# Giving each DMA engine an output region of its own in a bilinear-pairs kernel

## The chip, the cores and the metric

The kernel runs on one core of one Trainium2 chip. A core has five engines that run side by side: TensorE (PE, with its weight loads shown as PEld), VectorE (DVE), ScalarE (ACT), GpSimd (POOL) and SyncE (SP). Sixteen DMA engines move data between DRAM (HBM) and the core's on-chip memory (SBUF), which has 128 partitions. The metric is the time of one execution on the device, in microseconds (us). Before the change it is 766.56 us, the median of three runs (766.03 to 769.45). The profiled execution took 771.7 us, of which its profile spans 769.8.

## The reference

There are 1024 batch rows with 32 fields of 128 values each, and one 128 x 128 matrix for each of the 496 pairs of fields i < j. For every pair the first field's vector is multiplied by the pair's matrix, and the result, element by element, by the second field's vector:

```
v_i = inputs[:, I_IDX, :]
v_j = inputs[:, J_IDX, :]
transformed = jnp.einsum('bpd,ped->bpe', v_i, W)
return transformed * v_j
```

All is float32. The output has 1024 x 496 x 128 elements, 260 MB; the inputs have 17 MB (fields) and 33 MB (matrices). The kernel may choose its own layout in DRAM: the host only permutes axes before and after.

## The kernel before

**Layout.** The host hands the fields over as `xt` (128 elements d, 32 fields, 1024 batch rows) and the matrices as `wt`, four pairs to a block (124 blocks of 128 d x 4 pairs x 128 e). The output in DRAM is `(248, 128, 2, 1024)`: 248 groups g of two pairs (`OG = 2`), and in each group 128 rows e, one for each SBUF partition, of 2 pairs x 1024 batch rows. A group is thus one contiguous megabyte, and each partition's share of it, 8 KB, is contiguous too.

**Work.** Pairs are taken with i from 30 down to 0. A unit u is one pair q and one half h of the batch (512 rows). It has two parts:

- `first(u)` multiplies the pair's matrix with the field into a PSUM tile `po`. The first 15 pairs (`NATIVE = 5`) do so in one plain float32 matmul (L154). All others use a split in a rounded high part, a low part and a correction: two matmuls in the format float32r (L157), and then ScalarE scales the tile in place (L158).
- `second(u)`, `LAG = 3` units later, adds the third matmul (L166) and lets VectorE multiply `po` with the second field into the output tile `ot` (L172).

`split_w` (L94 to L97, ScalarE and GpSimd) and `split_x` (L109 to L115, and L195 on VectorE) make the parts. They are placed in the loop by a list with due times.

**Transfers.** The loop is written out in order (a manual schedule), and SyncE issues nearly all DMAs in it, in the order of the program: W blocks (256 KB, four blocks ahead), fields (512 KB), and after the fourth unit of each group the whole tile `ot[g]` (1 MB, L176). Only the last two pairs go out in four pieces of 256 KB (L174). Four `ot` tiles exist; VectorE can begin a group only once the output DMA of the fourth group before has landed.

**What the change touches.** Lines L174 and L176 name the target of the output DMAs; the rest is the declaration of the output tensor and the host's permutation after the run.

Of the kernel before, what the change touches and what calls it, by code (L numbers as in the profile page):

```python
# [1 line left out]

# [4 lines left out]

F32 = mybir.dt.float32
F32R = mybir.dt.float32r
ALU = mybir.AluOpType  # L10

P = 128
NF = 32
NQ = NF * (NF - 1) // 2
BT = 1024
HB = 512
WC = 2
WL = 4
OG = 2
EPS = 2.0**-12  # L20
NATIVE = 5
SHARED = 10
XDLAG = 10
LAG = 3
WLEAD = 4
XLEAD = 5


def _pairs():

    return [(i, j) for i in range(NF - 2, -1, -1) for j in range(i + 1, NF)]


@with_exitstack
def kernel(
    ctx: ExitStack,
    tc: tile.TileContext,
    xt: bass.AP,
    wt: bass.AP,
    out: bass.AP,  # L40
):

    nc = tc.nc
    pairs = _pairs()
    nchunk = NQ // WC  # L60

    xpool = ctx.enter_context(tc.tile_pool(name="x", bufs=1))
    spool = ctx.enter_context(tc.tile_pool(name="xs", bufs=2))
    rpool = ctx.enter_context(tc.tile_pool(name="wr", bufs=5))
    wpool = ctx.enter_context(tc.tile_pool(name="ws", bufs=4))
    opool = ctx.enter_context(tc.tile_pool(name="o", bufs=4))
    ppool = ctx.enter_context(tc.tile_pool(name="ps", bufs=8, space=bass.MemoryType.PSUM))

    x_sb = {}

    def load_x(f, n=1, pieces=1, eng=None):

        t = xpool.tile([P, n, BT], F32, tag=f"x{f}", name=f"x_{f}")
        s = BT // pieces
        for k in range(pieces):
            (eng or nc.sync).dma_start(out=t[:, :, k * s : (k + 1) * s], in_=xt[:, f : f + n, k * s : (k + 1) * s])
        for k in range(n):
            x_sb[f + k] = t[:, k, :]

    w_raw = {}  # L80

    def load_w(c, splits=(0, WL)):
        w_raw[c] = rpool.tile([P, WL, P], F32, tag="w", name=f"w_{c}")
        for a, b in zip(splits, splits[1:]):
            nc.sync.dma_start(out=w_raw[c][:, a:b, :], in_=wt[c, :, a:b, :])  # L85

    w_s = {}

    def split_w(c, u):

        k = c * WC % WL
        raw = w_raw[c * WC // WL][:, k : k + WC, :].rearrange("p q e -> p (q e)")
        h, l, d = [wpool.tile([P, WC * P], F32R, tag=t, name=f"{t}_{c}") for t in ("wh", "wl", "wd")]
        nc.scalar.mul(h, raw, 1.0 - 2.0**-13)  # L94
        nc.gpsimd.tensor_tensor(l, raw, h.bitcast(F32), ALU.subtract)  # L95
        nc.gpsimd.tensor_scalar(d, h.bitcast(F32), EPS, 1.0, ALU.mult, ALU.mult)  # L96
        nc.gpsimd.tensor_tensor(d, l.bitcast(F32), d.bitcast(F32), ALU.subtract)  # L97
        w_s[c] = (h, l, d)

    x_s = {}  # L100
    later = []

    def split_x(f, a, u):

        if a == 0:
            x_s[f] = [spool.tile([P, BT], F32R, tag=t, name=f"{t}_{f}") for t in ("xh", "xl", "xd")]
        s = slice(a, a + HB)
        h, l, d = [t[:, s] for t in x_s[f]]
        nc.scalar.mul(h, x_sb[f][:, s], 1.0 - 2.0**-13)  # L109
        nc.gpsimd.tensor_tensor(l, x_sb[f][:, s], h.bitcast(F32), ALU.subtract)  # L110
        nc.gpsimd.tensor_scalar(l, l.bitcast(F32), 1.0 / EPS, 1.0, ALU.mult, ALU.mult)  # L111
        if f > NF - 2 - NATIVE - SHARED:
            later.append((min(u + XDLAG, 2 * first_q[f] + LAG - 1), d, h.bitcast(F32), l.bitcast(F32)))
        else:
            nc.gpsimd.tensor_tensor(d, h.bitcast(F32), l.bitcast(F32), ALU.subtract)  # L115

    nq0 = NATIVE * (NATIVE + 1) // 2
    c0 = nq0 // WC
    first_q = {i: q for q, (i, j) in reversed(list(enumerate(pairs)))}

    todo = []
    for c in range(c0, nchunk):
        todo.append(((c - 3) * WC + 1, max(c * WC, nq0), lambda u, c=c: split_w(c, u)))
    for i in range(NF - 2 - NATIVE, -1, -1):
        for a in range(0, BT, HB):
            todo.append((first_q[i + 1] + 1 if i < NF - 3 - NATIVE else 2, first_q[i], lambda u, i=i, a=a: split_x(i, a, u)))
    todo.sort(key=lambda t: t[1])

    load_w(0, (0, 1, WL))
    load_x(NF - 2, pieces=2, eng=nc.scalar)
    load_x(NF - 1, pieces=2, eng=nc.scalar)
    load_x(NF - 3)
    load_x(NF - 4)
    load_w(1)
    for f in range(NF - 5, NF - 4 - XLEAD, -1):
        load_x(f)
    load_w(2)
    load_w(3)  # L140


    ctx.enter_context(tc.manual_schedule())
    po, ots = {}, {}


    def first(u):
        q, h = divmod(u, 2)
        i, c = pairs[q][0], q // WC
        r = slice(q % WC * P, (q % WC + 1) * P)  # L150
        s = slice(h * HB, (h + 1) * HB)
        po[u] = ppool.tile([P, HB], F32, tag="po", name=f"po_{u}")
        if q < nq0:
            nc.tensor.matmul(po[u], w_raw[q // WL][:, q % WL, :], x_sb[i][:, s], start=True, stop=True)  # L154
        else:
            for t in (0, 1):
                nc.tensor.matmul(po[u], w_s[c][t][:, r], x_s[i][t][:, s], start=t == 0, stop=t == 1)  # L157
            nc.scalar.mul(po[u], po[u], 1.0 + EPS)  # L158

    def second(u):  # L160
        q, h = divmod(u, 2)
        i, j = pairs[q]
        r = slice(q % WC * P, (q % WC + 1) * P)
        s = slice(h * HB, (h + 1) * HB)
        if q >= nq0:
            nc.tensor.matmul(  # L166
                po[u], w_s[q // WC][2][:, r], x_s[i][2][:, s], start=False, stop=True, skip_group_check=True
            )
        g, k = divmod(q, OG)
        if k == 0 and h == 0:  # L170
            ots[g] = opool.tile([P, OG, BT], F32, tag="ot", name=f"ot_{g}")
        nc.vector.tensor_tensor(ots[g][:, k, s], po.pop(u), x_sb[j][:, s], ALU.mult)  # L172
        if q >= NQ - 2:
            nc.sync.dma_start(out=out[g, :, k, s], in_=ots[g][:, k, s])  # L174
        elif k == OG - 1 and h == 1:
            nc.sync.dma_start(out=out[g], in_=ots[g])  # L176

    for u in range(2 * NQ + LAG):
        q = u // 2
        if u % (2 * WL) == 0 and (q // WL + WLEAD) * WL < NQ:  # L180
            load_w(q // WL + WLEAD)
        if u < 2 * NQ:
            i, j = pairs[q]
            if u % 2 == 0 and j == i + 1 and 0 <= i - 2 - XLEAD:
                load_x(i - 2 - XLEAD)
            first(u)
        if u >= LAG:
            second(u - LAG)
        if u % 2 == 1:
            ready = [t for t in todo if t[0] <= q]  # L190
            if ready:
                ready[0][2](u)
                todo.remove(ready[0])
        while later and later[0][0] <= u:
            nc.vector.tensor_tensor(*later.pop(0)[1:], ALU.subtract)  # L195
    assert not todo and not later


# [25 lines left out]
```

## Time and profile before

| | before |
|---|---|
| time, median of 3 | 766.56 us |
| span of the profile | 769.8 us |
| PE busy | 722.7 us (94%) |
| VectorE busy | 632.0 us (82%) |
| ScalarE busy | 638.7 us (83%) |
| GpSimd busy | 593.2 us (77%) |
| moved by the DMA engines | 310.11 MB, mean 403 GB/s |
| written to HBM, read from it | 260.05 MB, 49.28 MB |
| an output DMA (1 MB), issue to landing | 8.9 us |

PE's busy time is modelled, since matmuls overlap in the array. The page's second part cuts the span into 40 equal slices; a digit is the busy share in tenths, and the line named DMA is the mean over the sixteen DMA engines. The third part gives each DMA queue's share of these engines' time. The fourth follows the work that ended last back to the start; a share of it for a DMA means that something waited for that transfer. The fifth groups instructions by line. A packet is the piece that one DMA engine moves at a time, one 8 KB partition row for the output; the trace has a record of each packet's start, length and size.

### The profile page before, as it was taken

The page shows a single profiled execution, that of the slowest core. Times are in us where ns is not written, and L with a number is a line of the kernel's source. Part 1 is how long each engine was busy: PE and PEld are TensorE (multiplying, and loading weights), DVE is VectorE, ACT ScalarE, POOL GpSimd, SP SyncE. Part 2 cuts the span into 40 slices and gives each one's busy share as a digit, 9 for nine tenths or more (in the row PEclk, how much of TensorE's full clock was granted, in tenths as well). Part 3 has the DMA queues.
Part 4 walks back from the last instruction along what each step waited for, and adds up shares of the span by engine and source line. Part 5 has one row for each costly group of instructions (what it writes and reads, how often), then busy time and mean ns, then how long its engine had stood idle before and what let it go on. Part 6 is the DMA issues. An engine that isn't in the chain of part 4 may idle for free.

```text
span 769.8 us, 11824 instructions
## 1 busy us (share of the span) xinstructions
PE 722.7 (94%) x2946; PEld 545.4 (71%) x2946; DVE 632.0 (82%) x1012; ACT 638.7 (83%) x1256; POOL 593.2 (77%) x863
## 2 busy tenths in 40 slices
PE   7988999999999999999999989999999999999994
PEld 3556766677777676777777767777777777777773
DVE  4869888888888788888888878888888888888885
ACT  2276988888888898888888889998988898998983
POOL 2677998887889878878878696978786969697660
PEclk9999999999999999999999999999999999999998
DMA  9999999999999999999999999999999999999997
GB/s 352 424 419 384 407 397 410 405 400 406 410 405 403 400 409 416 409 379 421 411 414 407 412 403 406 411 407 408 415 410 395 408 410 409 409 408 405 400 401 307
DMA packets 59108, 310.11 MB, mean 403 GB/s; under 512 B 6560, under 2 KB 6816, under 8 KB 27424
## 3 DMA queue, kind: packets, MB, share of 16 engines
q1 hardware_dynamic: 58464, 308.31, 99.4%
q10 hardware_dynamic: 576, 1.05, 0.4%
q8 instruction: 24, 0.39, 0.2%
q14 instruction: 44, 0.36, 0.1%
HBM read 49.28 MB, written 260.05 MB: 402 GB/s over the span
## 4 chain that ended last, share of the span: by engine, by line
DMA 61%; DVE 21%; PE 15%; issue 2%; DVEq 0%; SPq 0%; ACT 0%
DMA out_dram<-ot 60%; DVE ot L172 19%; PE po L157 9%; PE po L166 4%; DVE xd L195 2%; PE po L154 1%; DMA x<-in_xt_dram 1%; DVEq L172 0%; SPq L85 0%; DVEq L217 0%; ACT po L158 0%; DVEq L195 0%
## 5 line engine op out<-in xcount | busy, mean ns | idle before, releaser
L172 DVE TENSOR_TENSOR ot<-po,x 128x512 f32<-128x512 f32 x992 | 618.6, 684 | 129.5 <-DMA out_dram<-ot 70.2
L158 ACT ACTIVATE po<-po 128x512 f32<-128x512 f32 x962 | 551.2, 583 | 106.5 <-PE po L157 53.3
L157 PE MATMUL po<-xh,wh 128*128 128x512 f32 x962 | 388.7, 404 | 24.4 <-DVE ot L172 21.6
L166 PE MATMUL po<-xd,wd 128*128 128x512 f32 x962 | 376.9, 392 | 5.7 <-DVE xd L195 5.7
L157 PE MATMUL po<-xl,wl 128*128 128x512 f32 x962 | 377.6, 392 | 2.2 <-POOL wl L95 2.1
L157 PEld LDWEIGHTS po<-xh,wh 128*128 128x128 f32 x962 | 180.9, 188 | 110.2 <-DVE ot L172 72.5
L95 POOL TENSOR_TENSOR wl<-w,wh 128x256 fp32r<-128x256 f32 x241 | 179.2, 744 | 92.1 <-ACT wh L94 90.7
L166 PEld LDWEIGHTS po<-xd,wd 128*128 128x128 f32 x962 | 181.0, 188 | 46.3 <-ACT po L158 3.8
L157 PEld LDWEIGHTS po<-xl,wl 128*128 128x128 f32 x962 | 181.1, 188 | 36.8 <-POOL wl L95 4.5
L97 POOL TENSOR_TENSOR wd<-wl,wd 128x256 fp32r<-128x256 f32 x241 | 180.0, 747 | 20.1
L96 POOL TENSOR_SCALAR wd<-wh 128x256 fp32r<-128x256 f32 x241 | 99.1, 411 | 20.3
L94 ACT ACTIVATE wh<-w 128x256 fp32r<-128x256 f32 x241 | 99.2, 412 | 0.5 <-DMA w<-in_wt_dram 0.5
L110 POOL TENSOR_TENSOR xl<-x,xh 128x512 fp32r<-128x512 f32 x52 | 67.3, 1293 | 19.8 <-ACT xh L109 19.5
L115 POOL TENSOR_TENSOR xd<-xh,xl 128x512 fp32r<-128x512 f32 x32 | 41.4, 1292 | 2.7
L109 ACT ACTIVATE xh<-x 128x512 fp32r<-128x512 f32 x52 | 32.5, 628 | 10.5 <-DMA x<-in_xt_dram 10.3
L111 POOL TENSOR_SCALAR xl<-xl 128x512 fp32r<-128x512 f32 x52 | 32.8, 631 | 4.6
L154 PE MATMUL po<-x,w 128*128 128x512 f32 x60 | 29.0, 645 | 4.1 <-DMA x<-in_xt_dram 4.1
L154 PEld LDWEIGHTS po<-x,w 128*128 128x128 f32 x60 | 12.1, 206 | 20.2 <-issue 13.9
L195 DVE TENSOR_TENSOR xd<-xh,xl 128x512 fp32r<-128x512 f32 x20 | 16.6, 831 | 0.0
L109 ACT ACT_TABLE_LOAD x1 | 1.3, 1283 | 2.6 <-issue 2.6
L211 POOL MEMSET const-float32-0.0<- 128x1 f32 x1 | 0.1, 98 | 0.2 <-issue 0.2
L211 POOL MEMSET const-bfloat16-1.0<- 128x1 bf16 x1 | 0.1, 101 | 0.0
(2 smaller groups left out, 0.2 us busy)
## 6 DMA issues: line engine op xcount, KB each, us to landing
out_dram<-ot SPq DMA_DIRECT2D x247, 1024.0 KB, 8.9
w<-in_wt_dram SPq DMA_DIRECT2D x123, 256.0 KB, 9.1
x<-in_xt_dram SPq DMA_DIRECT2D x30, 512.0 KB, 9.5
x<-in_xt_dram ACTq DMA_DIRECT2D x4, 256.0 KB, 5.1
out_dram<-ot SPq DMA_DIRECT2D x4, 256.0 KB, 7.0
w<-in_wt_dram SPq DMA_DIRECT2D x1, 192.0 KB, 3.6
w<-in_wt_dram SPq DMA_DIRECT2D x1, 64.0 KB, 2.9
```

Source lines behind the costliest of these rows:

```text
L94: nc.scalar.mul(h, raw, 1.0 - 2.0**-13)
L95: nc.gpsimd.tensor_tensor(l, raw, h.bitcast(F32), ALU.subtract)
L96: nc.gpsimd.tensor_scalar(d, h.bitcast(F32), EPS, 1.0, ALU.mult, ALU.mult)
L97: nc.gpsimd.tensor_tensor(d, l.bitcast(F32), d.bitcast(F32), ALU.subtract)
L109: nc.scalar.mul(h, x_sb[f][:, s], 1.0 - 2.0**-13)
L110: nc.gpsimd.tensor_tensor(l, x_sb[f][:, s], h.bitcast(F32), ALU.subtract)
L115: nc.gpsimd.tensor_tensor(d, h.bitcast(F32), l.bitcast(F32), ALU.subtract)
L154: nc.tensor.matmul(po[u], w_raw[q // WL][:, q % WL, :], x_sb[i][:, s], start=True, stop=True)
L157: nc.tensor.matmul(po[u], w_s[c][t][:, r], x_s[i][t][:, s], start=t == 0, stop=t == 1)
L158: nc.scalar.mul(po[u], po[u], 1.0 + EPS)
L166: nc.tensor.matmul(po[u], w_s[q // WC][2][:, r], x_s[i][2][:, s], start=False, stop=True, skip_group_check=True)
L172: nc.vector.tensor_tensor(ots[g][:, k, s], po.pop(u), x_sb[j][:, s], ALU.mult)
```

## The change

The output tensor becomes two-dimensional: 16 regions (`NE`), each of 3,968 x 1024 floats (15.5 MB) followed by a padding of 9 x 1024 floats (36 KB) that nobody writes. Region n holds partitions 8n to 8n+7 of every group, group after group. So one output DMA writes 64 KB into each of the sixteen regions, and in a region the next group follows directly on the one before. The purpose is that each of the sixteen DMA engines writes into a region of its own, in one continuous stream over the whole run, with regions that start at different offsets. Tiles, order of work, sizes of DMAs and arithmetic stay the same; the host undoes the new layout.

```diff
+NE = 16
+PAD = 9 * BT
...
         if q >= NQ - 2:
-            nc.sync.dma_start(out=out[g, :, k, s], in_=ots[g][:, k, s])
+            nc.sync.dma_start(out=out[:, g, :, k, s], in_=ots[g][:, k, s])
         elif k == OG - 1 and h == 1:
-            nc.sync.dma_start(out=out[g], in_=ots[g])
+            nc.sync.dma_start(out=out[:, g], in_=ots[g])
...
-    args.append(nc.dram_tensor("out_0_dram", (NQ // OG, P, OG, BT), F32, kind="ExternalOutput").ap())
+    own = NQ * P // NE * BT
+    whole = nc.dram_tensor("out_0_dram", (NE, own + PAD), F32, kind="ExternalOutput").ap()
+    args.append(whole[:, :own].rearrange("n (g e k b) -> n g e k b", g=NQ // OG, e=P // NE, k=OG))
...
-    y[:, perm, :] = got.transpose(3, 0, 2, 1).reshape(BT, NQ, P)
+    got = got[:, :own].reshape(NE, NQ // OG, P // NE, OG, BT)
+    y[:, perm, :] = got.transpose(4, 1, 3, 0, 2).reshape(BT, NQ, P)
```

## Prediction

> **What bounds the kernel now.** I read the page from its slices first, then the queues, the chain, the groups, and last the waits and two windows of the trace.
>
> ```profile
> DMA  9999999999999999999999999999999999999997
> GB/s 352 424 419 384 407 397 410 405 400 406 410 405 403 400 409 416 409 379 421 411 414 407 412 403 406 411 407 408 415 410 395 408 410 409 409 408 405 400 401 307
> DMA packets 59108, 310.11 MB, mean 403 GB/s; under 512 B 6560, under 2 KB 6816, under 8 KB 27424
> ...
> q1 hardware_dynamic: 58464, 308.31, 99.4%
> ...
> HBM read 49.28 MB, written 260.05 MB: 402 GB/s over the span
> ...
> DMA out_dram<-ot 60%; DVE ot L172 19%; PE po L157 9%; PE po L166 4%; DVE xd L195 2%; PE po L154 1%; DMA x<-in_xt_dram 1%; DVEq L172 0%; SPq L85 0%; DVEq L217 0%; ACT po L158 0%; DVEq L195 0%
> ...
> out_dram<-ot SPq DMA_DIRECT2D x247, 1024.0 KB, 8.9
> ```
>
> The reader is to see that all sixteen DMA engines are busy in every slice, that one queue fills 99.4% of their time, that 260 of 310 MB are the output, and that the output's DMAs are 60% of the chain. The kernel is bound by its transfers from start to end. The question for any change is therefore what it does to the time of one output packet. In the trace's records of single packets, the output goes in 31,664 packets of 8 KB: half of them take 309 ns, the mean is 319.8. That is 8192 B / 309 ns = 26.5 GB/s for each engine, and 424 GB/s for sixteen.
>
> The next bound lies close. A window late in the span, and the waits for output buffers:
>
> ```profile
> 500.00:600.00 100.00, 98.43 (x413) 76.02 (x412) 85.80 (x139) 90.44 (x179) 79.17 (x116) 1.00 1.01 408
> ```
>
> ```profile
> DVE ot L172 <- DMA out_dram<-ot: 70.2, 83, 2.1
> ```
>
> VectorE waits only 70.2 us in all for a free output buffer, and PE is 98.43% busy by the page's modelled ends. Matmuls start 0.227 us apart in the timeline, so 3 x 962 of them need 655 us, the 60 native ones at 645 ns 39 us; the chain's first matmul starts at 7.9 us, and the last output needs some 9 us to land: about 711 us is a floor under which no faster transfer takes the kernel.
>
> [...] The page counts eight packets to an engine and output DMA (31,664 / 247 / 16 = 8.0)[...]. No view shows which partition an engine reads[...].
>
> **The change, part by part.**
>
> *Bytes, packets and issues.* Still 247 DMAs of 1 MB and four of 256 KB at the end, from the same tiles in the same order. Each SBUF partition still holds 8 KB, so I expect the same 8 KB packets [...]: 0 us. The padding is never written: 0 us. If a DMA with two different shapes takes SyncE longer to issue, the queue hides it: an output lands 8.9 us after its issue, in a rhythm of two outputs per 5.78 us (VectorE's waits for a buffer in the timeline are at 610.10 and 615.89).
>
> *What the writes gain.* The most that a better DRAM layout can give is what packets take beyond their usual time: 31,664 x 10.8 ns / 16 = 21.3 us for the output, and 26.9 us with both kinds of loads. Some 17 us of this comes in short bursts, and late in the span these stand just ahead of a W load, where the engines turn from writing the output to reading; a new place for the output leaves that turn as it is. That leaves 10 us that could go. Value taken: 0 to 5 us, with 27 us as the outer end.
>
> *What DRAM can lose.* Sixteen streams now lie 15.5 MB + 36 KB apart. [...] Before, an output's sixteen shares all lay inside 1 MB. Value: 0, upper end 2% of the output's time (12 us).
>
> *Who reads which partitions.* This is the step on which I stake the forecast. The DRAM side's slowest dimension is now 16 and no longer 128. [...] Two engines [...] take about 2 x 309 = 618 ns for a packet.
>
> How much of the time partners are in step decides the size. [...] In the window from 600 to 606 us, in slices of 0.15 us, the bytes by start of packet go up and down:
>
> ```profile
> GB/s 601 218 614 177 683 137 737 109 492 273 109 68 273 478 369 423 751 232 519 232 628 232 601 273 601 218 601 218 655 164 655 218 601 273 546 328 492 382 492 382
> ```
>
> High and low alternate because most engines begin their packets in the same half of each 309 ns. Their offsets there are within half a packet; at 200 and 400 us they are spread over a whole one, with a few engines two to four packets ahead. [...]
>
> The output's packet time on one engine is 247 x 8 x 309 ns = 611 us; all of it lies on the bounding path, because the engines are never idle. Doubling all of it would add 611 us (1378 us). With a share of 0.5 it is 766.6 + 306 = 1073, with 0.87 it is 766.6 + 532 = 1299. Loads are untouched: their DRAM side keeps its shape. I take 0.7, as slow pairs hold up all others[...]: 766.6 + 0.7 x 611 = 1194, about 1195 us. VectorE would then wait for buffers at every output, PE behind it.
>
> **The rivals.**
>
> *No change (766 us).* [...] partners separate by four packets and stay so, and the DRAM layout was not limiting. For it: half of the packets are already at 309 ns, so the layout has little to mend. [...]
>
> *Faster (757 us).* One stream per engine removes the scattered part of the stalls, up to 10 us: 766.6 - 9.6. For it: mean above median by 10.8 ns per packet. Against it: most of the excess is at turns to a load.
>
> *Slightly slower (785 us).* Partners separate for the most part, with collisions left for some 3% of the output (611 x 0.03 = 18 us), or sixteen distant streams cost DRAM 2 to 3%. For it: offsets differ by a packet or more in mid-span. Against it: the late window shows them drawn together again.
>
> **How the numbers follow.** Sustained collisions 0.46, no change 0.22, faster 0.17, slightly slower 0.15. The likeliest is 1195 us. Slower is 0.46 + 0.15 = 0.61, within 0.5% 0.22, faster 0.17. Since the cases lie far apart, the range must hold two of them: from 758 (most of the faster case left out) to the full doubling's 1380.
>
> **What would show it.** For the forecast: output packets of 500 to 620 ns (the queue's share still near 100% while GB/s falls to about 260), 8 KB packets in unchanged number, VectorE's wait for the output grown from 70.2 us to several hundred, and landing of an output well over 8.9 us. [...] If packets change in number, the step "same packets" is wrong. If packets grow while the loads' packets grow too, DRAM is at fault[...]. The prediction is most easily wrong through the split itself[...], or through partners that fall out of step by themselves.

## The result, and the profile after

The changed kernel is slower: 843.23 us (median of four runs) against 767.35 us, a ratio of 1.099 (95% interval 1.091 to 1.108). The direction was the forecast one; the size was not, 76 us where 428 were forecast.

The page of the changed kernel, the lines that answer to those of before:

```profile
DMA  9999999999999999999999999999999999999998
GB/s 363 365 380 343 375 360 375 368 371 366 362 373 384 369 372 384 354 355 377 364 364 371 365 368 367 365 360 361 374 359 376 359 366 367 348 365 370 366 367 332
DMA packets 59108, 310.11 MB, mean 366 GB/s; under 512 B 6560, under 2 KB 6816, under 8 KB 27424
...
q1 hardware_dynamic: 58464, 308.31, 99.4%
...
DMA out_dram<-ot 71%; DVE ot L174 17%; PE po L159 4%; PE po L168 2%; DVE xd L197 1%; DMA x<-in_xt_dram 1%; POOL xl L112 1%; DMA w<-in_wt_dram 0%; POOL xl L113 0%; DVEq L174 0%; POOL wl L97 0%; ACT xh L111 0%; DVEq L221 0%; ACT wh L96 0%; POOL wd L98 0%
...
out_dram<-ot SPq DMA_DIRECT2D x247, 1024.0 KB, 10.5
```

The same number of packets and the same bytes, the same 99.4% of the DMA engines' time, and yet the rate falls from 403 to 366 GB/s in every slice alike. So single packets became slower. An output now lands 10.5 us after its issue instead of 8.9. VectorE's wait for a free output buffer grows from 70.2 us in 83 waits to:

```profile
DVE ot L174 <- DMA out_dram<-ot: 116.4, 110, 3.2
```

The late window that the prediction showed, with PE now less busy (98.43 before) and 364 GB/s instead of 408 at the same DMA share:

```profile
500.00:600.00 100.00, 92.91 (x375) 68.61 (x374) 76.54 (x124) 82.98 (x160) 69.91 (x105) 0.99 1.01 364
```

And the six microseconds in slices of 0.15 us, in which high and low alternated before. Now they do so only here and there: most of the time the engines no longer begin their packets together.

```profile
GB/s 328 492 273 369 191 410 259 464 259 451 300 464 382 369 410 451 382 437 382 437 437 382 437 355 519 341 464 396 492 273 451 355 410 218 396 369 492 287 478 369
```

The packet records say which packets became slower. The output's 8 KB packets have a mean of 359.4 ns instead of 319.8, while their median is still 309. The loads' packets hardly move: 2 KB 87.2 ns (86.1 before), 4 KB 164 ns (173). Four fifths of the output's packets take at most 320 ns (88% before); 12% take over 500 ns, and 146 over a microsecond (none before). The growth explains the time: 31,666 x 39.6 ns / 16 = 78 us, which is what lies between the spans of the two profiles (769.8 and 847.8); between the medians it is 76.

The one added cost on an issuing engine is this: an output DMA occupies SyncE for longer, now that its DRAM side has 16 rows and no longer the 128 of the SBUF side (332 ns again with 128 far regions, 559 with close shares, both below). Before, then after (ns, lowest/median/highest):

```profile
L176 SPq DMA_DIRECT2D out_dram<-ot x247: 332/332/1258, 14.3 to 759.0; - x124
```

```profile
L178 SPq DMA_DIRECT2D out_dram<-ot x247: 538/558/2527, 13.5 to 835.9; - x124
```

That is 0.23 us more for an output every 3 us or so. With the DMA engines busy throughout it should cost nothing, and with stores alone, below, the whole change costs 2.3 us.

### The profile page after: what moved, and what is told of

It is laid out like the page before. It is cut to its first block, busy times and chain, and to the rows that moved or that the text cites. A ratio compares the mean times of both kernels' runs of the same rounds, so it can differ in the third digit from the quotient of the medians.

```text
span 847.8 us, 11824 instructions
## 1 busy us (share of the span) xinstructions
PE 752.0 (89%) x2946; PEld 544.7 (64%) x2946; DVE 632.6 (75%) x1012; ACT 649.6 (77%) x1256; POOL 594.1 (70%) x863
## 2 busy tenths in 40 slices
DMA packets 59108, 310.11 MB, mean 366 GB/s; under 512 B 6560, under 2 KB 6816, under 8 KB 27424
## 3 DMA queue, kind: packets, MB, share of 16 engines
q1 hardware_dynamic: 58464, 308.31, 99.4%
## 4 chain that ended last, share of the span: by engine, by line
DMA 72%; DVE 18%; PE 6%; issue 1%; POOL 1%; DVEq 0%; ACT 0%; SPq 0%; POOLq 0%
DMA out_dram<-ot 71%; DVE ot L174 17%; PE po L159 4%; PE po L168 2%; DVE xd L197 1%; DMA x<-in_xt_dram 1%; POOL xl L112 1%; DMA w<-in_wt_dram 0%; POOL xl L113 0%; DVEq L174 0%; POOL wl L97 0%; ACT xh L111 0%; DVEq L221 0%; ACT wh L96 0%; POOL wd L98 0%
## 5 line engine op out<-in xcount | busy, mean ns | idle before, releaser
L159 PE MATMUL po<-xh,wh 128*128 128x512 f32 x962 | 401.4, 417 | 74.1 <-DVE ot L174 68.8
L159 PEld LDWEIGHTS po<-xl,wl 128*128 128x128 f32 x962 | 183.3, 191 | 28.8 <-issue 0.2
L99 POOL TENSOR_TENSOR wd<-wl,wd 128x256 fp32r<-128x256 f32 x241 | 178.1, 739 | 20.1
L98 POOL TENSOR_SCALAR wd<-wh 128x256 fp32r<-128x256 f32 x241 | 99.4, 413 | 20.3
## 6 DMA issues: line engine op xcount, KB each, us to landing
out_dram<-ot SPq DMA_DIRECT2D x247, 1024.0 KB, 10.5
```

## The experiments

### The place in DRAM, or the split

By the split the texts mean the rows into which the DRAM side of an output DMA falls: 128 before, 16 after. The forecast assumed that under the new split engines come in pairs (partners) that hold each other up while they run in step, and called that a collision. No view shows which engine takes which row or partition, nor what two of them would meet at, so this was my assumption. Of what was expected of the first three kernels, one figure holds if the split is to blame, the other if the place in DRAM is (the DRAM theory, or equal offsets).

Two kernels take the change apart. The first keeps the split of before (128 rows on both sides) and only moves the output into 128 far regions; the second keeps the new split (16 rows) and only brings the sixteen shares together again. The third is the changed kernel without its padding.

```diff
 (row regions)
-NE = 16
+NE = 128
```

> Only the place in DRAM changes: 128 regions, one for each partition, 1.94 MB + 36 KB apart; the DRAM side's slowest dimension is 128 as before the change[...]. [...] 8 KB packets at a mean near 320 ns, 767 us within 1%. DRAM theory (streams far apart slow the writes): at least as slow as the changed kernel, 840 us or more, packets near 360 ns.

```diff
 (close shares)
-    own = NQ * P // NE * BT
-    whole = nc.dram_tensor("out_0_dram", (NE, own + PAD), ...)
-    args.append(whole[:, :own].rearrange("n (g e k b) -> n g e k b", ...))
+    own = P // NE * OG * BT
+    whole = nc.dram_tensor("out_0_dram", (NQ // OG, NE, own + PAD), ...)
+    args.append(whole[:, :, :own].rearrange("g n (e k b) -> n g e k b", ...))
```

> Only the split changes: sixteen rows of 64 KB + 36 KB, as in the changed kernel, but all shares of a group lie together inside 1.6 MB and the next group follows. [...] 843 us within 1.5%, packets near 360 ns. DRAM theory: about 767 us, packets near 320 ns.

```diff
 (no padding)
-PAD = 9 * BT
+PAD = 0 * BT
```

> The changed kernel without the 36 KB of padding: regions exactly 15.5 MB apart. [...] 843 us within 1.5%. If regions at equal offsets fall on each other in DRAM: over 860 us.

| kernel | us | ratio to before (95%) | 8 KB packet, mean |
|---|---|---|---|
| row regions | 767.97 | 0.999 (0.997 to 1.001) | 316.4 ns |
| close shares | 843.48 | 1.100 (1.093 to 1.107) | 359.5 ns |
| no padding | 843.01 | 1.096 (1.092 to 1.099) | 358.5 ns |

Row regions, then close shares, from their pages:

```profile
DMA packets 59108, 310.11 MB, mean 405 GB/s; under 512 B 6560, under 2 KB 6816, under 8 KB 27424
```

```profile
DMA packets 59108, 310.11 MB, mean 369 GB/s; under 512 B 6560, under 2 KB 6816, under 8 KB 27424
```

The whole slowdown comes with the split, and none with the place in DRAM: neither far regions nor their offsets matter here. One thing on the DRAM side changes together with the split: each of the sixteen rows is now 64 KB in one piece. That this alone is slow is ruled out below, where stores with the same pieces take 634.3 us, 2.3 more than in the old layout.

### What engines in step cost

Stores alone, with all products left out, show the price without anything else in the way. `ot` is filled by VectorE from one field, four buffers as in the kernel.

```diff
+    for g in range(NQ // OG):
+        ot = opool.tile([P, OG, BT], F32, tag="ot", name=f"ot_{g}")
+        nc.vector.tensor_copy(ot[:, 0, :], xa[:, 0, :])
+        nc.vector.tensor_copy(ot[:, 1, :], xa[:, 0, :])
+        nc.sync.dma_start(out=out[g], in_=ot)      # new layout: out[:, g]
```

> Leaves out all products: the 248 output DMAs alone, from four tiles filled with copies of one field, DRAM layout of before the change. 247 x 8 packets x 309 ns is 611 us, with start and end 620 to 635 us under each theory.

> Leaves out all products: the 248 output DMAs alone, from four tiles filled with copies of one field, DRAM layout and split of the changed kernel. [...] partners that stay in step while nothing disturbs them: packets near 618 ns, 1100 to 1250 us. [...] partners that separate by themselves: packets near 309 ns, 620 to 680 us. DRAM theory: some 13 to 20% over the same stores in the old layout, spread over all packets and the whole span.

```diff
 (64 partitions)
-        nc.sync.dma_start(out=out[g], in_=ot)
+        nc.sync.dma_start(out=out[g, 0:64], in_=ot[0:64])
+        nc.sync.dma_start(out=out[g, 64:128], in_=ot[0:64])
```

> Leaves out all products: as many stored bytes, but each group is stored as two DMAs of 512 KB that both read partitions 0 to 63, in the old layout and split. [...] every 8 KB packet near 610 ns, 1200 to 1250 us. If two engines [...] don't hinder each other: 632 us, as with 128 partitions.

With 64 partitions as many bytes took 1281 us; a packet took 617 ns in the mean, 628 in the median. From its page:

```profile
DMA packets 39980, 260.96 MB, mean 204 GB/s; under 512 B 7968, under 2 KB 7968, under 8 KB 8224
...
q1 hardware_dynamic: 39968, 260.87, 96.3%
```

The engines' time is taken up (96.3%), and they move half of what they do with all 128 partitions (632.0 us, 315.2 ns a packet, below). A packet takes twice the usual 309 ns here, though the layout in DRAM is that of before. The prediction's 618 ns is right for this stream, and my upper limit for this run was 31 us too low. These DMAs are also half as large; DMAs of that size over all 128 partitions were not run, so it is not shown apart what the 64 partitions do.

The stores with all 128 partitions took 632.0 us in the old layout and 634.3 in the new. So the new split alone costs next to nothing, and the start of the trace shows why. Windows of the new layout; after the sum of the window the columns are VectorE and GpSimd, the clock, the share of the DMA engines and GB/s:

```profile
8.00:10.00 2.00, 1.70 (x3) 0.00 (x0) 1.00 0.88 176
10.00:12.00 2.00, 0.00 (x0) 0.00 (x0) 1.00 1.08 340
12.00:14.00 2.00, 1.29 (x2) 0.00 (x0) 1.00 0.97 373
14.00:16.00 2.00, 0.00 (x0) 0.00 (x0) 1.00 1.02 414
16.00:20.00 4.00, 2.33 (x4) 0.00 (x0) 1.00 1.00 418
```

The old layout in the first of these windows:

```profile
8.00:10.00 2.00, 1.61 (x3) 0.00 (x0) 1.00 0.96 393
```

All engines start together, busy, at half the rate, and reach the full one within some 7 us. In packets: the first 64 take 613 ns in the mean, the next 449, then 354, 340, 321, 313, and it stays at 311 to 316 (old layout: 325, 324, then 312 to 320). In step, packets take just what was forecast for engines that hold each other up (618 ns); but within three DMAs it is over, and it does not come back. This is what my prediction denied.

The packet records show how it ends. For every output DMA the trace has sixteen packets of 4 bytes, which I read as one behind each engine's share (the page of the whole kernel counts 6560 packets under 512 B for its 410 DMAs, 16 to each). In the old layout the engines reach the end of the first output within 0.15 us of each other. In the new one they begin it within 0.26 us and end it between 11.1 and 12.2 us, so the shares were not equal. Then the ends drift apart and come to rest: at each of 22 moments from 120 to 560 us the sixteen ends form eight pairs some 1.24 us apart, which is four packets, with a mean deviation of 14 to 118 ns (sixteen random moments, paired as well as they can be, would miss it by some 230). A lag of four packets is the one that the prediction names in its rival "no change"; why it is four was not shown.

This also tells what the alternating slices of the trace of before are worth. The new layout, from 300 to 306 us, at 419 GB/s:

```profile
GB/s 218 601 273 437 437 382 437 328 546 328 546 273 601 273 546 328 546 273 601 273 546 273 546 273 601 218 601 273 437 437 328 546 328 492 382 492 382 492 382 492
```

High and low alternate here too, with packets at their usual 311 to 316 ns. The pattern shows that engines begin packets at the same moments, not how many whole packets one is ahead of another.

### What keeps the long packets up in the whole kernel

If stores alone heal, something in the kernel must break them up again. The first suspect was the W load between stores. To the stores alone I added one, ahead of every second store:

```diff
+        if g % 2 == 0:
+            wb = rpool.tile([P, WL, P], F32, tag="w", name=f"w_{g}")
+            nc.sync.dma_start(out=wb, in_=wt[g // 2])
```

> Leaves out all products: the stores of before in the old layout, and one W block of 256 KB loaded ahead of every second store, in the kernel's order. By the packets at their usual length 632 us + 124 x 8 x 84 ns = 715 us, and some 0.15 us for each turn to a load as in the kernel before: 725 to 745 us under each theory.

> Leaves out all products: the same stores and W loads, with the split and regions of the changed kernel. Theory that loads bring partners back into step[...]: collisions return after every load, some 75 us over the same kernel in the old layout, 800 to 820 us. Rival (collisions come from the compute engines' waits and gaps in the issue, not from loads): within 10 us of the old layout.

712.7 us in the old layout and 820.4 in the new: the loads alone bring the long packets back, and no product is needed for it. In the old layout I had expected 725 to 745 us; the time is that of the packets at their usual length (715), so the turn to a load costs nothing of its own here. The pages, old and new:

```profile
DMA packets 53867, 293.45 MB, mean 413 GB/s; under 512 B 5984, under 2 KB 5984, under 8 KB 22112
```

```profile
DMA packets 53867, 293.45 MB, mean 358 GB/s; under 512 B 5984, under 2 KB 5984, under 8 KB 22112
```

What about a load does it? Its turn, whatever its size; its bytes, on their way into the SBUF that stores read; or its duration, in which one partner still stores and the other doesn't. Three edits tell these apart: loads of 32 KB, copies from DRAM to DRAM, and two halves of 128 KB.

```diff
 (small loads)
-            nc.sync.dma_start(out=wb, in_=wt[g // 2])
+            nc.sync.dma_start(out=wb[:, 0:1, 0:64], in_=wt[g // 2][:, 0:1, 0:64])
 (DRAM copies)
-            nc.sync.dma_start(out=wb, in_=wt[g // 2])
+            nc.sync.dma_start(out=spare[g // 2 % 8], in_=wt[g // 2])
 (half loads, ahead of every store)
+        wb = rpool.tile([P, 2, P], F32, tag="w", name=f"w_{g}")
+        nc.sync.dma_start(out=wb, in_=wt[g // 2, :, g % 2 * 2 : g % 2 * 2 + 2])
```

> Leaves out all products: stores in the old layout, and ahead of every second store a load cut to an eighth of a W block (32 KB). By packets 632 + 124 x 8 x 18 ns = 650 us under each theory, 640 to 665.

> Leaves out all products: the same stores and loads of 32 KB, with the split and regions of the changed kernel. Theory that the turn to a load puts partners back into step, whatever its size: 60 to 110 us over the old layout, 710 to 760 us. Rival[...]: an eighth of the 108 us seen with whole blocks, 14 us over the old layout, 660 to 670 us.

> Leaves out all products: stores in the old layout, and in place of each W load a copy of the same 256 KB from DRAM to DRAM, so an engine is away from the stores as long and reads DRAM, but nothing is written to SBUF. 632 + 124 x 0.62 us = 709 us, up to 740, under each theory.

> Leaves out all products: the same with the split and regions of the changed kernel. Theory that partners slip out of phase because one is away for 0.65 us while the other still stores: 70 to 110 us over the old layout. Theory that loaded bytes on their way into SBUF meet the stores' reads[...]: within 15 us of the old layout.

> Leaves out all products: stores in the old layout, and ahead of every store half a W block (128 KB), so the same bytes in twice as many loads. As with whole blocks, 713 us, up to 735.

> Leaves out all products: the same with the split and regions of the changed kernel. Slip theory: each load slips partners half as far and small slips are healed (a load of an eighth cost nothing), so 20 to 80 us over the old layout. Bytes theory: the same bytes cost the same 108 us over the old layout.

| stores and ... | old, us | new, us | new - old | 8 KB packet, old and new |
|---|---|---|---|---|
| nothing | 632.0 | 634.3 | 2.3 | 315.2, 315.5 ns |
| 124 loads of 32 KB | 641.1 | 643.2 | 2.2 | 312.4, 313.0 ns |
| 248 loads of 128 KB | 710.1 | 750.5 | 40.4 | 310.1, 332.4 ns |
| 124 loads of 256 KB | 712.7 | 820.4 | 107.7 | 313.4, 361.7 ns |
| 124 copies of 256 KB, DRAM to DRAM | 711.1 | 806.4 | 95.3 | 313.6, 364.1 ns |

The small loads refute my theory that each turn puts partners into step. The copies put no byte into SBUF and cost nearly as much as the loads, which refutes the rival of the loaded bytes. What is left is my reading, which agrees with all five rows: a long enough piece of other work between the stores (eight packets of 84 ns, the median of a 2 KB packet, are 0.67 us, over two store packets) lets one partner store while the other doesn't, and shifts their phase. The run with copies shows such a shift: the ends of the engines' shares lie in two groups, and no longer 1.24 us apart but 1.8 to 1.9, four packets and one copy of 0.61 us. With the loads of 256 KB no such order was found in the records, and by the theory both partners run the same loads, so the way from a load to a collision is not shown step by step. These are single runs. The differences of 95 and 108 us are far above what the runs of any one kernel here differ by (48 us at most, with the halved loads below); the 40 us of the half loads are not, and bear less.

### The same in the whole kernel

Here the loads were paired (two blocks at once, half as often), and then halved.

```diff
 (paired)
-        if u % (2 * WL) == 0 and (q // WL + WLEAD) * WL < NQ:
-            load_w(q // WL + WLEAD)
+        if u % (4 * WL) == 0:
+            for c in range(max(q // WL + WLEAD - 1, WLEAD), min(q // WL + WLEAD + 1, NQ // WL)):
+                load_w(c)
 (halved)
+        if u % WL == 0 and (q // WL + WLEAD) * WL < NQ:
+            load_half(q // WL + WLEAD, u // WL % 2)
```

> The kernel before with its W blocks loaded two at a time, half as often; layout and split as before. If each turn from stores to a load costs 0.15 us, some 9 us less: 758 us; if the later arrival of some blocks delays the splits of W, up to 770 us.

> The changed kernel with its W blocks loaded two at a time, half as often. Theory that loads bring partners into step: the 76 us of collisions fall by the share of turns taken away, 62 of 154, to some 46 us over the old layout with paired loads, about 805 us. Rival (collisions are there whatever the loads do): still 76 us over it, 835 us.

> The kernel before with every W block loaded in two halves of 128 KB, one ahead of each output, the same bytes in all. [...] 767 us within 0.5%; at best 3 us less, as with stores and loads alone (712.7 against 710.1).

> The changed kernel with every W block loaded in two halves of 128 KB, one ahead of each output. Slip theory: the 76 us over the old layout fall as they did with stores and loads alone (from 108 to 40), to some 28 us, and the field loads, unchanged, keep a little more: 795 to 805 us. If the compute engines' waits keep up the collisions in the full kernel: still some 843 us.

Paired loads: 770.3 us in the old layout and 824.3 in the new (805 expected). The cost of the new split falls from 76 to 54 us, near the 46 expected: again it follows the loads. For the kernel before, the pairing brought no gain (ratio 1.004, 1.002 to 1.007) where I expected 9 us from fewer turns; that stores and loads alone lose nothing at the turns fits this.

Halved loads went against the expectation: 772.1 us in the old layout (ratio 1.008, 1.005 to 1.010) and 901.2 in the new, so the cost rose to 129 us. The four runs spread from 876 to 924 us, so the size is uncertain, but even the fastest is 104 us over the old layout. The slices of the page, from a run of 901 us, show more than the sum does:

```profile
GB/s 363 364 382 343 347 334 338 351 330 338 349 332 328 353 319 357 373 314 337 334 333 328 327 345 324 338 343 326 328 396 387 399 391 341 323 335 340 324 339 344
```

Four slices in the last third run at 387 to 399 GB/s, most others near 335. In packets it is a mean of 329 to 339 ns in that stretch and mostly 365 to 415 elsewhere. 332 is the mean of stores and half loads alone, nearly from start to end. Their slices:

```profile
GB/s 286 377 389 394 400 392 406 391 397 397 397 396 399 396 394 396 397 391 403 398 394 401 390 398 397 401 398 392 397 395 398 398 393 400 393 396 395 394 395 355
```

It looks as if the same pattern of stores and half loads has a good phase, which the bare pattern finds at once and keeps, and which the whole kernel finds once and loses again. What makes it lose the phase (fields that are loaded, or the less regular issue) was not tried. That loads between stores are enough to bring the long packets back is shown; how number and length of the loads set the size in the whole kernel, and what else there adds to it, stays open.

No experiment pointed to a version faster than the kernel before: the old split leaves its output packets at a mean of 316 to 320 ns whatever the place in DRAM.

## Why the prediction was right in direction and wrong in size

- *Bound by the output's transfers, so a packet's time decides.* Right: the growth of the packets explains the whole change.
- *Same number of packets, issue hidden.* Right: 59,108 packets, and 0.23 us more for each issue with at most 2.3 us to show for it (stores alone).
- *A new place in DRAM gains 0 to 5 us and loses 0.* Right: 0.999 with 128 far regions, and no loss without padding.
- *The split: engines in pairs that take 618 ns a packet in step.* An assumption, with twice the usual 309 ns as my estimate. What it foretells came: the slowdown comes with the split alone (1.100 against 0.999), the first packets of the new split take 613 ns, a packet takes 617 from 64 partitions, and undisturbed engines end their shares in pairs 1.24 us apart. Which engine read which partition, and what two of them meet at, was not shown.
- *Partners that stay in step, and so a share of 0.7.* This is the step that failed. How a lag turns into such a share was assumed too; no trace or run showed it. Sharing is not equal: in the first output of the stores alone, engines that begin within 0.26 us of each other end 1.1 us apart, and within three DMAs they have separated; what brings the long packets back is other work between the stores. The measured share, counted as if every collision cost a whole 309 ns, is 39.6 / 309 = 0.13, so the term that was put at 0.7 x 611 = 428 us came to 78. I read from the trace of before that most engines start their packets together, and took this for a small lag that would last under the new split. But starting together says nothing of whole packets, and before the change only 2.3% of the output's packets took over 500 ns (12% after), so that trace could hardly show what holding each other up does to the engines' lag. The rival called no change had the way out (partners four packets apart that stay so), which the stores alone take; the rival called slightly slower had what the whole kernel shows, engines that mostly don't hold each other up (80% of the output's packets take at most 320 ns), and put the share of the rest at 0.03.
- *A packet of 618 ns.* Right in the mean of a steady stream (617 ns, and no packet over 684, with 64 partitions), but not for every packet of the changed kernel: 3.4% take over 700 ns, up to 1.67 us, and hold 37 of the 78 us. Two engines that share equally would give 618 ns by that estimate, not such packets; what makes them that long was not found.
- *Slow pairs hold up all others, hence the upper part of the range.* Not seen: the engines are busy 99.4% of the span as before, and with 80% of the packets at their usual length none of them waits long for a slow one.
- *The range.* 758 to 1380 held the time only because it reached from one case to the other; the likeliest value was 352 us too high, and that 843 lies inside is luck.

Why the sharing is unequal was not found.

## What to carry to other kernels

A change of layout in DRAM can change more than the place. Here 16 rows in place of 128 on the DRAM side cost 10%, wherever the rows lay (843.2 and 843.5 us), and 128 far regions cost nothing (768.0); what was seen fits engines that hold each other up, but where they do was not shown. In a kernel like this one, keep 128 as the slowest dimension on both sides. When engines may hold each other up, don't reckon with the full doubling or with none (a share of 0.13 here, from 39.6 of 309 ns): look at what interrupts the stream, and measure the stream alone and then with its interruptions. A trace in which hardly any packet is held up (2.3% of the output's over 500 ns before the change) can't tell how engines will hold each other up.

## What the runs showed of the hardware that I had not expected

- In the new split sixteen engines, started in step, go from 613 to 313 ns a packet within three DMAs (some 9 us) and settle in pairs four packets apart, though nothing in the program orders them.
- A store stream in the new split is broken up by 0.67 us of other work every two stores (108 us over 124 loads, 0.87 us each) and not at all by loads of 32 KB (643.2 us against 641.1 in the old layout), each 0.14 us of work by an estimate of 18 ns a packet, on the line through the 27 ns of 512 B and the 84 ns of 2 KB (medians in the trace of before).
- Regions 15.5 MB apart without padding cost no more than with it (843.0 and 843.2 us).
